# A delta-rule attention block on one core: the rounds of a head laid out by hand, with the build-time scheduler switched off

## The chip, the cores and the metric

The kernel runs on one core of a Trainium2 chip, in 32-bit floating point throughout. The metric is the time of one execution in microseconds, as the device reports it; the median of several runs is given. The profiled execution is one further run, taken by the hardware profiler. Engines are called PE (matrix multiplication, TensorE), DVE (VectorE), ACT (ScalarE), POOL (GpSimd) and SP (SyncE, which here issues most of the DMAs).

## The reference

The input x has 8 batches of 256 tokens with 256 channels. A modulation of a small vector c gives six rows per batch. Cut to what matters:

```
mod = silu(c) @ wmod                    # sa, ca, ga, sb, cb, gb per batch
h = layernorm(x) * (1 + ca) + sa
x = x + ga * attention(h)
h = layernorm(x) * (1 + cb) + sb
x = x + gb * (sparsify_2to4(silu(h @ w_gate) * (h @ w_up)) @ w_down)

# attention: 16 key heads, two value heads for each, 128 wide
q, k, v = causal_conv_4_taps(h @ W_qkv);  q, k = l2norm(q), l2norm(k)
for t in range(256):                    # state S of each value head, 128 x 128
    dv = beta[t] * (v[t] - k[t] @ S)
    S = S * decay[t] + outer(k[t], dv)
    o[t] = q[t] @ S
y = (rms_norm(o) * norm_w * silu(h @ W_z)) @ W_out
```

`sparsify_2to4` keeps, of every four neighbouring hidden values, the two that are largest in magnitude.

## The kernel before

The recurrence is solved in chunks of 128 tokens, two per batch. Within a chunk the influence of a key on later ones is a triangular matrix of 128 x 128, which is inverted in blocks of 32; with the inverse, a chunk becomes a few 128-wide matmuls.

The 8 batches are taken in four pairs, and for each pair the 16 key heads in four groups of four (`GH = 4`). So the main loop (from L1058) runs over 16 groups and 64 heads; each head serves both batches of the pair, both chunks and both value heads.

The work is written as generators, each of which issues some instructions on several engines and then yields:

- `attend` (L753 to L880), one for each batch of the pair, six steps. Values are transposed (`ps_v` L767) and scaled on ACT (`vn` L772); keys are multiplied with keys and queries (`ps_kq` L779 to L783), scaled on ACT (`cross` L786) and DVE (`aq` L788); then `ps_u` L798 with its copy `u` L800; `ps_ks` L806 with `rr` L811 on DVE and `o` L820 on ACT, and `ps_o` L825 with its copy L826; `ps_u1` L831 with L833; last `ps_o1` L837, added to `o` by DVE (L838). After that comes the normalisation: squares on ACT (`junk`, `ss` L845), a scaling on DVE (`ss` L848), a power of -1/2 on POOL (`rs`, in the helper at L105), and four products on DVE (`og` L861). It leaves behind a generator `turned` (L870) that waits five rounds, transposes `og` (`ps_gt` L877) and scales it (`og_p` L878).
- `levels` (L658 to L750), the inverse of the head that comes next, four steps: loads of its blocks by SP (`x_even` L675, the diagonal of `t_inv` L676, `x_top` L681, `low_up` L685), `ps_w` L691 with the copies `w` L699, `ps_t` L705 with the transpose `low` L713 on DVE and copies on ACT, `ps_w2` L731/L734 with `w2` L738, `ps_t2` L742/L745 with the copies into `t_inv`.
- `prepare` (L606 to L655), the query, the two values and two gates of the head that comes next: `ps_qv` L432 with a convolution of one ACT instruction (L418) and three of DVE (L420), `ps_z` L634 with a SiLU (L641), and the norm of the query (`ps_n2q` L447, with squares `junk` L451 on ACT ahead of it).
- `shares` (L891, `ps_y`, added up on DVE in L902), the output projection of two heads, once in two heads.
- `ahead`, called the background: keys, decays and triangular matrices of the next group (`ps_k` L432, `ps_n2k` L447, `diag` L516 on POOL, a scan L551, `ps_kk` L532, `a_t` L563), then the 30 solving steps `tmp` L592 and `xb` L598 on DVE.
- the feed: either `other_filled`, which makes the modulated tokens of a later pair (`ps_h` L147 and others), or `feed_forward` (L160 to L256) of one unit of 128 tokens of the pair before: `ps_ff` L190, SiLU L197, product `hid` L198, magnitudes L205, comparisons L211 to L224, mask `hid` L229, `ps_out` L244, result L252 and L253. The last four units come after the main loop and run one step each in turn.

The program has eight PSUM banks in three pools: three for projections and `ps_y` (`ps_in`), two for the inverse and the feed-forward (`ps_inv`), three for `attend` and the rest (`ps_mix`). A pool's next user waits until the bank's reader is done.

What sets the order of the work: in each head a list of generators is stepped round and round (L1105 to L1127), in the order `turned` of the head before, the older `shares`, `attend` of batch 0, `attend` of batch 1, `levels`, `prepare`. After each round `along` (L1073) steps the background as far as a planned share of its work, and then the feed. A head has 7 or 9 rounds, a group 32. This written order is not yet the program: the context that builds it is called with `schedule_with_timeline_sim=True` (L1201), with which instructions are reordered at build time by a simulated timeline, dependencies kept.

## Time and profile before

| | |
|---|---|
| median of 3 runs | 2168.65 us (2167.95, 2168.65, 2175.1) |
| profiled execution | 2163.81 us |
| its span in the profile | 2162.0 us |
| granted PE clock, mean | 0.987 of full speed |
| instructions in the profile | 46431 |
| moved by DMA | 226.85 MB, 105 GB/s in the mean |
| POOL, largest groups | `rs` L105 135.2 us in 128 instructions, `diag` L516 122.8 us in 64 |

The profile calls an engine busy from the start of an instruction to its end. Matmuls are pipelined on PE, so that one begins before the last has ended, and their ends are modelled; weight loads are counted apart, as PEld. A wait is put down to the instruction that released it last ("releaser"). An entry such as `L105` is a line of the kernel, and `out<-in` gives the names of the tiles that an instruction writes and reads.

### The profile page before, as it was taken

Reading aid. Unit: us, or ns where it says so; the run is one execution under the profiler, and the core shown is the slowest. Engines: PE = TensorE matmul, PEld = TensorE weight load, DVE = VectorE, ACT = ScalarE, POOL = GpSimd, SP = SyncE. Lnnn points to the kernel's source line nnn. Section 1 sums busy time; section 2 is a strip of 40 time slices with the busy share of each in tenths; the row PEclk is TensorE's granted clock in tenths of the full one; section 3 lists DMA queues with packets and bytes.
Section 4 is the critical chain, followed back from the end, with each engine's and each line's share of the span. In section 5 each row is a group of like instructions: output and inputs, shape, how many; then the busy total and the mean of one; then the engine's idle time right before and its main releaser. Section 6 shows DMA issues by size and latency. Waiting matters only on the chain.

```text
span 2162.0 us, 46431 instructions
## 1 busy us (share of the span) xinstructions
PE 2061.9 (95%) x16684; PEld 1634.1 (76%) x16684; DVE 1663.1 (77%) x4039; ACT 1373.6 (64%) x4552; POOL 370.7 (17%) x375
## 2 busy tenths in 40 slices
PE   8889999999999999999999999999999989999998
PEld 5567777777777777778777787787878777787887
DVE  6688686877869578797878868788797868879457
ACT  3577676866656566666566656666676666666652
POOL 3120212112120111212121121211202012121010
PEclk9999999999999999999999999999999999999999
DMA  4242423333342443434434343443434344343336
GB/s 137 85 117 65 105 68 101 91 83 91 101 117 67 124 115 95 132 90 109 119 90 118 104 109 94 122 117 87 132 92 108 92 115 120 108 113 90 75 91 212
DMA packets 324517, 226.85 MB, mean 105 GB/s; under 512 B 254520, under 2 KB 266168, under 8 KB 324288
## 3 DMA queue, kind: packets, MB, share of 16 engines
q1 hardware_dynamic: 304416, 163.34, 28.2%
q10 hardware_dynamic: 19872, 60.54, 8.8%
q8 instruction: 133, 2.18, 0.4%
q14 instruction: 96, 0.79, 0.1%
HBM read 186.28 MB, written 29.12 MB: 100 GB/s over the span
## 4 chain that ended last, share of the span: by engine, by line
PE 64%; ACT 12%; DVE 11%; DMA 7%; issue 4%; SPq 1%; POOL 1%; ACTq 0%; DVEq 0%; POOLq 0%
PE ps_y L891 9%; PE ps_qv L432 8%; PE ps_z L634 8%; PE ps_ks L806 5%; PE ps_ff L190 3%; PE ps_k L432 3%; PE ps_o L825 2%; PE ps_u L831 2%; DVE cv L420 2%; PE ps_out L244 2%; DMA blk<-scr 2%; PE ps_kk L532 2%; DMA scr<-a_t 2%; PE ps_u L798 2%; DVE a_t L563 2%
## 5 line engine op out<-in xcount | busy, mean ns | idle before, releaser
L420 DVE SCALAR_TENSOR_TENSOR cv<-ps_qv,conv_sb,cv 128x510 f32<-128x510 f32 (+1 forms) x564 | 410.2, 737 | 43.5 <-ACT cv L418 39.4
L432 PE MATMUL ps_qv<-h_bp,wh 128*128 128x512 f32 x768 | 365.1, 601 | 12.0 <-ACT junk L451 8.4
L105 POOL TENSOR_TENSOR rs<-ss,minus_halves 128x4 f32<-128x4 f32 x128 | 135.2, 1058 | 1019.6 <-DVE ss L848 1018.6
L634 PE MATMUL ps_z<-wh,h_bp 128*128 128x256 f32 x1024 | 250.4, 390 | 9.5 <-ACT junk L451 6.6
L891 PE MATMUL ps_y<-wo,og_p 128*128 128x256 f32 x1024 | 236.8, 380 | 0.8 <-ACT og_p L878 0.8
L432 PEld LDWEIGHTS ps_qv<-h_bp,wh 128*128 128x128 f32 x768 | 133.3, 191 | 118.9 <-issue 99.3
L634 PEld LDWEIGHTS ps_z<-wh,h_bp 128*128 128x128 f32 x1024 | 189.1, 193 | 38.5 <-ACT junk L451 9.9
L891 PEld LDWEIGHTS ps_y<-wo,og_p 128*128 128x128 f32 x1024 | 187.4, 190 | 22.8 <-ACT og_p L878 1.1
L418 ACT ACTIVATE cv<-ps_qv,conv_sb 128x512 f32<-128x512 f32 x188 | 129.6, 690 | 117.6 <-PE ps_qv L432 117.0
L592 DVE TENSOR_TENSOR tmp<-blk,xb 128x30 f32<-128x30 f32 (+14 forms) x480 | 156.8, 327 | 57.8 <-ACT xb L586 48.7
L516 POOL TENSOR_TENSOR diag<-consts,bk 128x1032 f32<-128x1032 f32 x64 | 122.8, 1919 | 384.5 <-DVE bk L507 352.6
L845 ACT ACTIVATE junk<-o 128x128 f32<-128x128 f32 x512 | 153.3, 303 | 41.4 <-DVE o L838 35.0
L551 DVE TENSOR_TENSOR_SCAN e<-dbc,diag 128x1032 f32<-128x1032 f32 x60 | 137.9, 2298 | 39.3 <-POOL diag L516 36.3
L598 DVE TENSOR_TENSOR xb<-xb,tmp 128x30 f32<-128x30 f32 (+14 forms) x480 | 157.0, 327 | 9.5
L420 DVE SCALAR_TENSOR_TENSOR k_t<-ps_k,conv_sb,k_t 128x510 f32<-128x510 f32 (+1 forms) x189 | 139.7, 740 | 24.8 <-ACT k_t L418 22.9
L861 DVE SCALAR_TENSOR_TENSOR og<-o,rs,gz 128x128 f32<-128x128 f32 x512 | 145.9, 344 | 10.3 <-POOL rs L105 8.1
L772 ACT ACTIVATE vn<-ps_v,nk 128x256 f32<-128x256 f32 x256 | 106.2, 483 | 61.4 <-PE ps_v L767 61.2
L806 PE MATMUL ps_ks<-u,cross 128*128 128x128 f32 x1024 | 141.0, 280 | 0.9 <-ACT u L800 0.9
L806 PEld LDWEIGHTS ps_ks<-u,cross 128*128 128x128 f32 x1024 | 130.8, 194 | 9.5 <-issue 3.3
L190 PE MATMUL ps_ff<-h,w_ff 128*128 128x128 f32 x1024 | 130.0, 277 | 3.2 <-ACT h L149 2.2
L190 PEld LDWEIGHTS ps_ff<-h,w_ff 128*128 128x128 f32 x1024 | 122.5, 192 | 7.8 <-ACT h L149 3.2
L432 PE MATMUL ps_k<-h_bp,wk 128*128 128x512 f32 x256 | 124.9, 613 | 1.6 <-ACT junk L451 1.2
(177 smaller groups left out, 4274.8 us busy)
## 6 DMA issues: line engine op xcount, KB each, us to landing
wh<-in_w_heads ACTq DMA_DIRECT2D x64, 640.0 KB, 4.0
w_ff<-in_w_ff SPq DMA_DIRECT2D x128, 256.0 KB, 2.9
dbc<-d_dram SPq DMA_DIRECT2D x60, 516.0 KB, 4.3
wo<-in_w_heads ACTq DMA_DIRECT2D x32, 512.0 KB, 3.7
w_dn<-in_w_down SPq DMA_DIRECT2D x64, 256.0 KB, 3.8
wk<-in_w_keys SPq DMA_DIRECT2D x16, 512.0 KB, 4.5
scr<-a_t SPq DMA_DIRECT2D x256, 32.0 KB, 2.6
blk<-scr SPq DMA_DIRECT2D x16, 512.0 KB, 3.6
```

The lines of the kernel that those rows point to most:

```text
L105: nc.gpsimd.tensor_tensor(out=out, in0=in_, in1=minus_halves[:, :n], op=ALU.pow)
L190: nc.tensor.matmul(ps[:, a, l, :], lhsT=w[:, k, l, :], rhs=h2[:, k, :], start=(k == 0), stop=(k == CC - 1),)
L420: nc.vector.scalar_tensor_tensor(out=dst[:, :, d:], in0=ps[:, :, : T - d], scalar=taps[:, KC - 1 - d : KC - d], in1=dst[:, :, d:], op0=ALU ...
L432: nc.tensor.matmul(ps.rearrange("p b t -> p (b t)"), lhsT=w[k], rhs=h_bp[:, k, :], start=(k == 0), stop=(k == CC - 1),)
L551: nc.vector.tensor_tensor_scan(e.rearrange("p i s t -> p (i s t)"), dbc.rearrange("p i f -> p (i f)"), diag.rearrange("p s t -> p (s t)"), ...
L592: nc.vector.tensor_tensor(out=tmp, in0=blk[:, j, j + 1 :, None].to_broadcast([P, m, j]), in1=xb[:, j, None, 0:j].to_broadcast([P, m, j]), ...
L598: solved = nc.vector.tensor_tensor(out=xb[:, j + 1 :, 0:j], in0=xb[:, j + 1 :, 0:j], in1=tmp, op=ALU.subtract)
L634: nc.tensor.matmul(ps[:, n, :], lhsT=h_bp[:, k, i * T + n * P : i * T + (n + 1) * P], rhs=wh[:, k * 640 + 384 : (k + 1) * 640], start=(k = ...
L806: nc.tensor.matmul(ps_ks[:, ct, h, :], lhsT=cross[:, h, ct, :], rhs=u0[:, h, :], start=True, stop=True)
L845: nc.scalar.activation(junk, o[:, n, h, :], AF.Square, accum_out=ss[:, n, h : h + 1])
L861: nc.vector.scalar_tensor_tensor(out=og[:, n, h, :], in0=o[:, n, h, :], scalar=rs[:, 2 * n + h : 2 * n + h + 1], in1=gz[:, i, n, h, :], op ...
L891: nc.tensor.matmul(ps_y[:, n, :], lhsT=og_p[:, j // 2, i, n, j % 2, :], rhs=wo[:, j // 2, j % 2, :], start=(j == 0), stop=(j == 3),)
```

## The change

Two things are changed. The build-time scheduler's flag is set to False, and the order of a round is written anew. The generators of a head are now stepped in this order: `attend` of batch 0, `levels` (called `inverse`), `prepare` (called `queries`), `attend` of batch 1, the background, the feed, and last `turned` of the head before with the older `shares`. To allow that, `along` is divided into `next_group` and `feeding`, which `shares_of` turns into endless generators; the loop ends when all the others are used up.

```
-            def along():
-
-                nonlocal done, rounds, fed
+            def next_group():
+
+                nonlocal done, rounds
                 rounds += 1
                 while done < work * rounds / (total * 3 / 4):
...
+            def feeding():
+
+                nonlocal fed
                 while fed < (FEED_STEPS + LATER) * rounds / total:
...
-                turns, ends[:] = ends[:], []
+                turned, ends[:] = ends[:], []
                 if hp % 2 == 0:
-                    turns.append(waiting)
+                    turned.append(waiting)
...
-                turns += [attend(rec, i, *shared, t_inv[head % 2], og_p[:, hp % 2, i]) for i in range(2)]
+                atts = [attend(rec, i, *shared, t_inv[head % 2], og_p[:, hp % 2, i]) for i in range(2)]
...
-                    turns.append(levels(coming[0], *coming[1], t_inv[(head + 1) % 2]))
+                    inverse = levels(coming[0], *coming[1], t_inv[(head + 1) % 2])
...
-                        gen, shared = begin(to_come["kh"], to_come["bp"], to_come["h"])
-                        turns.append(gen)
-                while turns:
-                    with tc.issue_after(first_solved) if head == 0 else ExitStack():
-                        turns = [t for t in turns if next(t, turns) is not turns]
-                    along()
+                        queries, shared = begin(to_come["kh"], to_come["bp"], to_come["h"])
+                turns = [atts[0], inverse, queries, atts[1], shares_of(next_group), shares_of(feeding), *turned]
+                left = {id(t) for t in (*turned, *atts, inverse, queries)}
+                while left:
+                    for t in turns:
+                        with tc.issue_after(first_solved) if head == 0 else ExitStack():
+                            if next(t, turns) is turns:
+                                left.discard(id(t))
...
-    with tile.TileContext(nc, schedule_with_timeline_sim=True) as tc:
+    with tile.TileContext(nc, schedule_with_timeline_sim=False) as tc:
```

The number of instructions of each engine is the same in both programs, and so is the number of rounds of each head. In the built programs the order differs on every engine; counted as runs of equal neighbours, PE has 3246 rows before and 3355 after, DVE 3410 and 3618, ACT 2365 and 2394, POOL 323 and 365, SP 748 and 823. With the flag at False the built order is still not letter for letter the written one. An example from PE of the changed program, where four matmuls of one norm, 32-wide blocks of an inverse and a projection, each written in one piece, stand mixed:

```
L447 n2k x1
L691 ps_w x1
L447 n2k x3
L432 ps_k x1
L691 ps_w x15
```

More of the change, by code (lines that the diff above doesn't have):

```diff
@@ L1055, in later, with shares_of @@
             yield from gen
+        def shares_of(work):
+            while True:
+                yield work()
         og_p = wo = shared = None
@@ L1094, in adaln_block @@
                     for _ in levels(rec, *scratch, t_inv[head % 2]):
-                        along()
-                turns, ends[:] = ends[:], []
+                        next_group()
+                        feeding()
+                turned, ends[:] = ends[:], []
                 if hp % 2 == 0:
-                    turns.append(waiting)
+                    turned.append(waiting)
                     og_p = two.tile([P, 2, 2, NCH, 2, P], F32, tag="og_p", name="og_p", bufs=1)
@@ L1108, in adaln_block @@
                     waiting = shares(ya, k0 + hp == 0, og_p, wo, 6)
-                turns += [attend(rec, i, *shared, t_inv[head % 2], og_p[:, hp % 2, i]) for i in range(2)]
+                atts = [attend(rec, i, *shared, t_inv[head % 2], og_p[:, hp % 2, i]) for i in range(2)]
                 solved, coming = False, None
+                inverse = queries = iter(())
                 if hp + 1 < GH:
@@ L1118, in adaln_block @@
                     solved = True
-                    turns.append(levels(coming[0], *coming[1], t_inv[(head + 1) % 2]))
+                    inverse = levels(coming[0], *coming[1], t_inv[(head + 1) % 2])
                     if head > 0:
                         to_come = coming[0]
-                        gen, shared = begin(to_come["kh"], to_come["bp"], to_come["h"])
-                        turns.append(gen)
-                while turns:
-                    with tc.issue_after(first_solved) if head == 0 else ExitStack():
-                        turns = [t for t in turns if next(t, turns) is not turns]
-                    along()
+                        queries, shared = begin(to_come["kh"], to_come["bp"], to_come["h"])
[6 more added lines that the diff above has]
+                                left.discard(id(t))
                 head += 1
```

## The prediction

> **What bounds the kernel now.** I read the busy row first, then the shares of the chain that ended last, then PE's timeline inside one head, then PE's and DVE's waits, last the tail.

> ```profile
> PE 2061.9 (95%) x16684; PEld 1634.1 (76%) x16684; DVE 1663.1 (77%) x4039; ACT 1373.6 (64%) x4552; POOL 370.7 (17%) x375
> PE 64%; ACT 12%; DVE 11%; DMA 7%; issue 4%; SPq 1%; POOL 1%; ACTq 0%; DVEq 0%; POOLq 0%
> ```

> TensorE (PE) looks full, yet only 64% of the chain lies on it; ACT and DVE carry 23% and DMA 7%. The timeline of PE settles which of the two to believe:

> ```profile
> 1001.36 3.62 PE L891 MATMUL ps_y<-wo,og_p 128*128 128x256 f32 x16
> 1004.81 1.88 PE L432 MATMUL ps_k<-h_bp,wk 128*128 128x512 f32 x4
> 1006.53 0.60 PE L767 MATMUL ps_v<-consts,cv 128*128 128x128 f32 x4
> 1007.06 0.69 PE L691 MATMUL ps_w<-x_even,a_t 32*32 32x32 f32 x32
> ```

> A row's first column is its start, the second its length. Each row ends after the next has begun: 16 matmuls of 256 columns take 3.45 us from start to start, 216 ns each, where the page gives 380 as the mean of one. By starts I find 430 ns for 512 columns, 216 for 256, 111 for 128, 109 for transposes and norms, 20 and 29 for the 32- and 64-wide blocks. With the counts of the groups: 1024 x 430 + 2560 x 216 + 5120 x 111 + 1600 x 109 + 4096 x 20 + 2048 x 29 ns = 440 + 553 + 568 + 174 + 82 + 59 = 1,876 us; with some 30 us at the start for the first loads, about 1,910. So PE loses some 250 us of the 2,162, where its busy row leaves 100. [...] It matters for this sum: by the busy row a better order could win 100 us at the very most, by the starts up to 250, so a large gain can't be ruled out from "95%". About half of the lost time I find in named waits, about half in pieces of 0.1 us at changes of operand without a releaser. The named ones:

> ```profile
> PE ps_kq L779 <- ACT vn L772: 16.0, 11, 3.0
> PE ps_qv L432 <- ACT junk L451: 8.4, 10, 1.2
> PE ps_z L634 <- ACT junk L451: 6.6, 10, 0.9
> PE ps_w L731 <- ACT x_top L720: 4.2, 5, 1.3
> PE ps_t L705 <- ACT w L699: 2.3, 5, 0.6
> PE ps_t L705 <- DMA t_inv<-scr_y: 2.2, 2, 1.3
> PE ps_out L244 <- DVE hid L229: 0.2, 1, 0.2
> ```

> (us in all, times, longest.) They are few and short; the last rows are links that today hardly wait at all.

> **The change part by part.** No instruction is added or taken out: every engine has the same count of each kind, so PE's 1,910 us stand. What moves is order, and the built order of the changed program can be read. It is not the order written: neighbours still come mixed (four columns of one norm between pieces of an inverse), so I cost the built order. Method: for each link from a producer to a PE instruction I add up PE's work (durations above) that stands between them before and after, and compare it with the link's measured need. Sums are made against the profiled execution, 2163.81 us (span 2162.0 and 1.8 around it); the median shown, 2168.65, lies 4.8 above it.

> *What goes.* The norms of query and key no longer hold the three projection banks just ahead of L432 and L634: 8.4 + 6.6 + 1.2 = 16 us of waits on L451, between 0 and -20; I take -16. The second batch's ps_kq stands a whole turn of inverse and queries after its values: of the 16.0 us of L779, 0 to -16; the first batch's place is as tight as before, so -6.

> *The gap at POOL.* The normalisation goes DVE L848, POOL L105 (1,058 ns, 128 times), DVE L861. Today DVE works meanwhile:

> ```profile
> 1044.86 0.15 DVE L848 SCALAR_TENSOR_TENSOR ss<-ss,eps_q 128x4 f32<-128x4 f32 x1
> 1044.98 0.22 DVE L592 TENSOR_TENSOR tmp<-blk,xb 128x58 f32<-128x58 f32 x1
> 1045.23 0.22 DVE L598 TENSOR_TENSOR xb<-xb,tmp 128x58 f32<-128x58 f32 x1
> 1045.49 0.24 DVE L592 TENSOR_TENSOR tmp<-blk,xb 128x84 f32<-128x84 f32 x1
> 1045.77 0.25 DVE L598 TENSOR_TENSOR xb<-xb,tmp 128x84 f32<-128x84 f32 x1
> 1046.14 1.14 DVE L861 SCALAR_TENSOR_TENSOR og<-o,rs,gz 128x128 f32<-128x128 f32 x4
> ```

> Four solve steps fill the 1.13 us, so the wait of L861 on POOL sums to 8.1 us only. In the built order 115 of the 128 places have under 1 us of DVE work between L848 and L861 (half of them none): DVE idles some 85 us more. Queued behind each waiting L861 are the conv (L420) and the additions L838, for whose banks PE waits. DVE is only 77% busy, so most costs nothing; it tells where DVE's work per head exceeds PE's. After the change that is the fourth head of each group (DVE 21 us, PE 19). There 16 heads x 2 gaps x 0.9 = 28 us; half of it reaches PE: +14, between 0 and +60.

> *The feed-forward's output.* L244 needs the masked hidden L229. Before, 0.2 us. In the built order 8 of the 12 units inside the loop have 13.3 us of DVE work queued from the last transpose L713 to L229, and PE 11.4 us until L244: 8 x 1.9 = +15; overlapping with the gap above I take +10 for this and +12 for POOL's, bounds 0 and +25.

> *The tail.* The last four units run alone, with two banks:

> ```profile
> 2132.32 10.98 PE L190 MATMUL ps_ff<-h,w_ff 128*128 128x128 f32 x96 [0.92 <-DVE hid L198]
> 2143.74 5.45 PE L244 MATMUL ps_out<-w_dn,hid 128*128 128x256 f32 x24 [0.44 <-DVE hid L198]
> 2149.38 8.90 PE L244 MATMUL ps_out<-w_dn,hid 128*128 128x256 f32 x40 [0.19 <-DVE hid L229]
> ```

> PE waits 1.5 us here. In the built order eight of the masks L229 stand in one block ahead of five of the products L198 that free the banks: 4.9 us of DVE work against banks already used up. And from the last L198 to the first unit's own last L229 lie 6.5 us of DVE work against 1.7 us of PE work (eight matmuls of L244): another 4.8. Some of it stands before too, so +8, between +3 and +12. Such a gap has a second price. [...] In this trace PE is idle 5.12 us before L470 at 62.30, and the granted clock reads 0.76 in 60:64, 0.81 in 64:68 and 1.00 after: 0.24 x 4 + 0.19 x 4 = 1.7 us lost. By the row 1.7 for a gap of 5 us, [...] I add 2 for the tail, which makes it +10. [...]

> *The inverse.* PE work between the copy w (L699) and L705 is under 1.2 us in 19 of 64 heads (11 before), between w2 (L738) and its products (L742) in 20 (5 before). 23 more tight places at about 0.25 us, the mean of the rows above being 0.5: +6 (0 to +12). The inverse's loads: L676 lands 1.9 us after issue in the median, queued on SP behind others; the cover of L705 falls below 4 us in 24 heads, none before. At 0.2 each +5 (0 to +15).

> *Banks of the attention.* From the last addition L838 to the bank's next user PE now has under 1 us of work in 43 heads (never under 2 before), and DVE needs 0.5 to 1.45: 43 x 0.12 = +5 (0 to +25). In exchange the conv's banks get longer cover (5.6 us at the fifth percentile, 3.7 before), which is in the -16 already.

> *More changes.* PE's rows of equal neighbours grow from 3,246 to 3,355. At 0.05 us, the loss without a releaser over the rows: +5 (0 to +14).

> *The start.* The modulation copy L406, which must wait for PE's L399 (10.25 us), comes ahead of some of the statistics, so xs L137 and the first transposes L147 slip: +2 (0 to +4).

> Sum: -16 - 6 + 12 + 10 + 10 + 6 + 5 + 5 + 5 + 2 = +33. 2163.8 + 33 = 2196.8; the median of such runs lies up to 4.8 higher. I say 2199.

> **The rivals.** *DVE becomes the bound.* The 85 us of gaps and the fourth heads' 21 against 19 us add up instead of hiding: every group hands a lag on. With the upper ends for POOL's gap (+60), the output (+25), the banks (+15) and the rest as above the sum is +90: about 2250. For it: 77% busy over the span, and DVE's queue runs in the order built. Against: in the other three heads of a group PE has 5 to 12 us more work than DVE, and the lag is caught up.

> *Faster.* Spreading the two batches' steps round the inverse and the queries lets each eviction hide, and of the 125 us of unnamed small losses and the 50 us named a part vanishes: -22 for what I name, and a fifth of the rest, -25, with the costs above at their lower ends (about +10): 2163.8 - 37, about 2130. It decides if DVE never lags more than the 2 to 3 us cover it has; the longer cover of u0 (2.2 to 2.6 us at the lower quartile) and of the gates (2.6 to 4.1) speak for it, the thinner covers above against.

> *It does not do what it says.* Part of the order is still the builder's, the counts and rounds are the same, and gains and losses cancel: 2168, plus or minus 6.

> **How the numbers follow.** About 0.3% is what a measurement can tell from no change: 2162.1 to 2175.2. The sum of the terms 0.50, DVE as the bound 0.22, no change 0.11, faster 0.17. The likeliest case alone spans 2178 to 2225 (the terms' bounds, not all at one end). The range reaches from 2150, inside the faster case, to 2255, the DVE case's middle and a little: some 2 in 10 stay outside. Faster 0.17, same 0.11, slower 0.72.

> **What would show it.** PE's waits on junk L451 all but gone; og L861 on POOL's rs up from 8.1 to some 90 us; new PE rows ps_out on hid L229 (about 15 us), ps_ff on hid L198 in the tail, ps_v on o L838, ps_t on w L699 and on t_inv; a clock slice under 1.00 in the tail; ps_h starting near 13 us, not 11.40. Wrong if L861's row stays near 10, or if PE's idle without a releaser shrinks while the named rows stay as short as before.

## The result and the profile after

The changed kernel takes 2249.41 us in the median of four runs (2239.8 to 2255.21), beside 2169.48 for the kernel before on the same chips (2167.95 to 2175.1): 1.0359 times as long, with an interval of 1.0318 to 1.0400. It is 80 us slower; the sum of the forecast was 33. Its profiled execution took 2255.21 us, with a span of 2253.1, so 91 us of span are to be explained, beside the 2162.0 of before.

The busy row of the page for the changed kernel:

```profile
PE 2112.9 (94%) x16684; PEld 1650.6 (73%) x16684; DVE 1639.7 (73%) x4039; ACT 1357.6 (60%) x4552; POOL 368.6 (16%) x375
```

The counts of PE, DVE, ACT and POOL are those of before. PE's busy time has grown by 51 us without one more matmul, which already says that "busy" is not work: the same matmuls took longer, or their ends were held back. The chain of this trace could be followed over 13% of the span only, so I don't use it.

PE's waits in the changed kernel (us in all, times, longest):

```profile
PE ps_n2k L447 <- DVE k_t L420: 22.1, 15, 2.0
PE ps_out L244 <- DMA w_dn<-in_w_down: 16.1, 8, 4.0
PE ps_u L831 <- ACT o L820: 13.9, 11, 2.2
PE ps_u L798 <- ACT vn L772: 8.8, 7, 2.2
PE ps_t L705 <- ACT w L699: 7.2, 3, 4.2
...
PE ps_qv L432 <- ACT junk L451: 1.7, 4, 0.4
PE ps_k L432 <- ACT junk L451: 1.2, 1, 1.2
```

The first three of them in the kernel before:

```profile
PE ps_u L831 <- ACT o L820: 0.6, 1, 0.6
...
PE ps_out L244 <- DMA w_dn<-in_w_down: 0.5, 2, 0.3
PE ps_n2k L447 <- DVE k_t L420: 0.5, 1, 0.5
```

The waits of before are gone: L779 on vn (16.0 us) is not in the list at all, the three on junk L451 (16 us) are down to 2.9. In their place stand others that come back at one place of nearly every group: the norm of the fourth key (15 waits in 15 of the 16 groups), the feed-forward's weights (8 in 12 units). The bank that ps_u1 takes from ps_ks adds 11 waits.

DVE's timeline round one normalisation (L848 and L861 are the scaled sum and the products; the bracket is the idle time ahead, and its releaser):

```profile
1070.78 0.16 DVE L848 SCALAR_TENSOR_TENSOR ss<-ss,eps_q 128x4 f32<-128x4 f32 x1
1072.06 1.14 DVE L861 SCALAR_TENSOR_TENSOR og<-o,rs,gz 128x128 f32<-128x128 f32 x4 [1.12 <-POOL rs L105]
```

Where four solve steps filled the 1.13 us before, DVE now stands idle, and a second time right behind (1.15 us ahead of 1074.42). The list of DVE's waits sums it, first in the changed kernel, then in the kernel before:

```profile
DVE o L838 <- PE ps_o L837: 118.0, 56, 6.8
DVE og L861 <- POOL rs L105: 105.6, 104, 1.2
```

```profile
DVE o L838 <- PE ps_o L837: 42.6, 24, 4.0
...
DVE og L861 <- POOL rs L105: 8.1, 12, 1.1
```

The tail of PE in the changed kernel:

```profile
2196.11 13.61 PE L190 MATMUL ps_ff<-h,w_ff 128*128 128x128 f32 x116
2216.17 13.00 PE L190 MATMUL ps_ff<-h,w_ff 128*128 128x128 f32 x96 [6.45 <-DVE hid L198]
2229.00 3.62 PE L244 MATMUL ps_out<-w_dn,hid 128*128 128x256 f32 x16
2236.64 12.31 PE L244 MATMUL ps_out<-w_dn,hid 128*128 128x256 f32 x48 [4.03 <-DVE hid L229]
```

The two waits forecast at 4.9 and 4.8 are 6.45 and 4.03 us. And the same 96 matmuls that took 10.98 us take 13.00, right behind the wait. Why they do is told by the windows of the profile: length, busy time of PE with its number of instructions, and PE's granted clock (the last two columns are of the DMAs).

```profile
1052.00:1056.00 4.00, 2.34 (x27) 1.00 0.56 153
1056.00:1060.00 4.00, 3.90 (x16) 0.57 0.19 33
1060.00:1064.00 4.00, 4.00 (x35) 1.00 0.13 21
...
2212.00:2216.00 4.00, 0.00 (x0) 0.70 0.07 27
2216.00:2220.00 4.00, 3.83 (x18) 0.50 0.14 44
```

The first three rows lie round one wait of 1.76 us on the fourth key (PE goes on at 1056.10): in the next four microseconds PE is busy for 3.90 and gets through 16 instructions, at a clock of 0.57. A clock of 0.50 stands in the records in stretches of 3.41 us or a multiple, called half-clock windows below: 57 us in all before, 103 after.

With the trace's start times all 91 us can be sorted. From each PE instruction to the next I take off the time that its shape needs at full speed (the durations of the forecast) and put what is left into one of four classes: over 150 ns with a releaser that the trace names; a change of tile size on PE (128 to 32 or 64 wide or back); within a stretch at half clock; the rest. In us, with the number of size changes and of half-clock windows of 3.41 us:

| kernel (its profiled span) | named waits | half clock | size changes | rest |
|---|---|---|---|---|
| before (2162) | 114 | 22 (17) | 58 (550) | 36 |
| changed (2253) | 158 | 43 (30) | 67 (624) | 54 |
| difference | +44 | +20 | +9 | +18 |

PE's work is 1,921 us in both, close to the 1,910 of the forecast. Half of the loss is waits with a name. Nearly a quarter is a slower clock behind such waits, for which the forecast had 2 us.

### The profile page after: what moved, and what is told of

Read it like the earlier page. It is cut to its first block, busy times and chain, and to the rows that moved or that the text cites. A ratio compares the mean times of both kernels' runs of the same rounds, so it can differ in the third digit from the quotient of the medians.

```text
span 2253.1 us, 46385 instructions
## 1 busy us (share of the span) xinstructions
PE 2112.9 (94%) x16684; PEld 1650.6 (73%) x16684; DVE 1639.7 (73%) x4039; ACT 1357.6 (60%) x4552; POOL 368.6 (16%) x375
## 5 line engine op out<-in xcount | busy, mean ns | idle before, releaser
L420 DVE SCALAR_TENSOR_TENSOR cv<-ps_qv,conv_sb,cv 128x510 f32<-128x510 f32 x564 | 416.4, 739 | 55.8 <-ACT cv L418 53.5
L432 PE MATMUL ps_qv<-h_bp,wh 128*128 128x512 f32 x768 | 386.1, 615 | 3.9 <-DVE y L902 2.2
L105 POOL TENSOR_TENSOR rs<-ss,minus_halves 128x4 f32<-128x4 f32 x128 | 133.6, 1044 | 1020.7 <-DVE ss L848 1020.7
L634 PE MATMUL ps_z<-wh,h_bp 128*128 128x256 f32 x1024 | 257.9, 394 | 0.0
L861 DVE SCALAR_TENSOR_TENSOR og<-o,rs,gz 128x128 f32<-128x128 f32 x512 | 153.8, 347 | 117.3 <-POOL rs L105 105.6
L891 PE MATMUL ps_y<-wo,og_p 128*128 128x256 f32 x1024 | 234.2, 384 | 0.0
L891 PEld LDWEIGHTS ps_y<-wo,og_p 128*128 128x128 f32 x1024 | 193.2, 193 | 33.0 <-ACT og_p L878 5.9
L516 POOL TENSOR_TENSOR diag<-consts,bk 128x1032 f32<-128x1032 f32 x64 | 122.8, 1918 | 554.3 <-DVE bk L507 546.8
L634 PEld LDWEIGHTS ps_z<-wh,h_bp 128*128 128x128 f32 x1024 | 188.9, 196 | 24.8 <-issue 0.9
L772 ACT ACTIVATE vn<-ps_v,nk 128x256 f32<-128x256 f32 x256 | 107.2, 476 | 148.5 <-PE ps_v L767 148.3
L432 PEld LDWEIGHTS ps_qv<-h_bp,wh 128*128 128x128 f32 x768 | 127.6, 192 | 82.0 <-issue 67.3
L592 DVE TENSOR_TENSOR tmp<-blk,xb 128x30 f32<-128x30 f32 (+14 forms) x480 | 156.3, 326 | 15.1 <-ACT xb L586 12.0
L598 DVE TENSOR_TENSOR xb<-xb,tmp 128x30 f32<-128x30 f32 (+14 forms) x480 | 156.7, 327 | 3.5
L420 DVE SCALAR_TENSOR_TENSOR k_t<-ps_k,conv_sb,k_t 128x510 f32<-128x510 f32 (+2 forms) x189 | 135.7, 734 | 31.0 <-ACT k_t L418 30.1
L838 DVE TENSOR_TENSOR o<-o,ps_o 128x256 f32<-128x256 f32 x128 | 53.1, 419 | 122.8 <-PE ps_o L837 118.0
L190 PE MATMUL ps_ff<-h,w_ff 128*128 128x128 f32 x1024 | 129.7, 280 | 10.3 <-DVE hid L198 6.5
L190 PEld LDWEIGHTS ps_ff<-h,w_ff 128*128 128x128 f32 x1024 | 123.1, 195 | 18.9 <-DVE hid L198 7.3
L432 PE MATMUL ps_k<-h_bp,wk 128*128 128x512 f32 x256 | 132.5, 619 | 4.2 <-ACT gz L641 3.0
```

The lines of the kernel that those rows point to most:

```text
L105: nc.gpsimd.tensor_tensor(out=out, in0=in_, in1=minus_halves[:, :n], op=ALU.pow)
L190: nc.tensor.matmul(ps[:, a, l, :], lhsT=w[:, k, l, :], rhs=h2[:, k, :], start=(k == 0), stop=(k == CC - 1),)
L420: nc.vector.scalar_tensor_tensor(out=dst[:, :, d:], in0=ps[:, :, : T - d], scalar=taps[:, KC - 1 - d : KC - d], in1=dst[:, :, d:], op0=ALU ...
L432: nc.tensor.matmul(ps.rearrange("p b t -> p (b t)"), lhsT=w[k], rhs=h_bp[:, k, :], start=(k == 0), stop=(k == CC - 1),)
L592: nc.vector.tensor_tensor(out=tmp, in0=blk[:, j, j + 1 :, None].to_broadcast([P, m, j]), in1=xb[:, j, None, 0:j].to_broadcast([P, m, j]), ...
L598: solved = nc.vector.tensor_tensor(out=xb[:, j + 1 :, 0:j], in0=xb[:, j + 1 :, 0:j], in1=tmp, op=ALU.subtract)
```

## The experiments

Theory A: the flag is the cause. Without the simulated timeline each engine's order has fixed places in every group where too little lies between producer and consumer, and the half clock follows the waits. Theory B: one of these, DVE idle on POOL ahead of L861, makes DVE the bound. Theory C: the new layout of the round is the cause. Ratios are to the kernel before, run on the same chip, with their intervals.

**Flag and layout apart.** One kernel has the round as before and the flag at False:

```
-    with tile.TileContext(nc, schedule_with_timeline_sim=True) as tc:
+    with tile.TileContext(nc, schedule_with_timeline_sim=False) as tc:
```

> The round written as before, only the scheduler's flag set to False. Theory A (the loss is the flag's: without the simulated timeline DVE's L861 stands right behind L848, loads and evictions stand at fixed, too short distances in every group): as slow as the changed kernel or slower, 2240 to 2300 us, with L861's wait on POOL at some 105 us again (the built order has under 1 us of DVE work in 124 of the 128 gaps). Theory C (the loss is the new layout's: both batches apart, the background in the middle): close to before, 2165 to 2190. If the layout makes good a part of what the flag costs, this is slower than 2249.

The other has the new layout and the flag left at True.

> The new layout of a round with the scheduler's flag left at True. Theory A: within 1% of before, 2155 to 2190 us, L861's wait on POOL well under 105 us (the built order fills 55 of the 128 gaps with over 1 us, against 80 before), and few gaps of PE over 1.2 us. Theory C: near the changed kernel, 2225 to 2255.

The flag alone: 2239.41 us, 1.0337 (1.0295 to 1.0379), as slow as the changed kernel within the intervals. The layout alone: 2149.99, 0.9919 (0.9886 to 0.9951), faster than before. C is out: the layout wins 0.8% with the scheduler, and without it the two layouts can't be told apart. The flag is what costs: 3.4% on the old layout, 4.4% on the new one (1.0359 by 0.9919). By the classes of the table the flag alone has 151, 39 (29 windows), 68 and 60, the layout alone 108, 20 (15), 57 and 37. The waits of DVE in the kernel with the flag alone, then in that with the layout alone:

```profile
DVE og L861 <- POOL rs L105: 119.8, 124, 1.2
```

```profile
DVE og L861 <- POOL rs L105: 36.0, 36, 1.2
```

So POOL's place ahead of L861 is a mark of the flag too. In the kernel with the flag alone the chain that ended last can be followed over the whole span:

```profile
PE 51%; DVE 24%; ACT 9%; DMA 7%; POOL 4%; issue 4%; SPq 1%; ACTq 0%; POOLq 0%; DVEq 0%
```

Before it was PE 64%, DVE 11% and POOL 1%. So with the flag off DVE stands on the chain for a quarter of the time, though it is busy for only 73% of the span; POOL itself takes a small part. Whether POOL's place is what costs, the next runs ask.

**DVE and POOL.** First attempt, one yield ahead of the products:

```
+            yield
             og = mixp.tile([P, NCH, 2, P], F32, tag="og", name="og", bufs=2)
```

> The changed kernel with one yield ahead of the four products L861, so that they are written a turn later than POOL's power and DVE has other work between. Theory B (DVE is the bound, fed by its idle time on POOL): L861's wait falls from 105.6 us to under 40, and the time by 30 to 60 us, to about 2200. Theory A (DVE's idle time on POOL is mostly slack; PE loses at other places, a few us each, and by the lower clock after each): the wait falls as much, the time by less than 15 us, 2235 to 2250.

2243.78 us, 1.0358 (1.0324 to 1.0393). It says nothing for or against: the wait was still 102.6 us in 108 places (104 in the changed kernel), so in these places of the built order, which with the flag off is not the written one either, too little work stood between the power and the products. Second attempt, the power left out:

```
-            rs = small.tile([P, NS], F32, tag="rs", name="rs")
-            rsqrt(rs, ss.rearrange("p n h -> p (n h)"))
+            rs = ss.rearrange("p n h -> p (n h)")
```

> The changed kernel without POOL's power of -1/2 on the sums of squares (L861 multiplies by the scaled sum itself; the power is left out of the computation), so that DVE's L861 has nothing to wait for behind L848. The yield of the run before did not do that: L861's wait stayed at 102.6 us. Theory B (DVE's idle time on POOL, 105.6 us, is what makes PE late): 30 to 60 us less, about 2200. Theory A (it is slack, PE loses at fixed places of the order and by the half clock behind them): less than 15 us, 2235 to 2250.

2209.45 us, 1.0211 (1.0187 to 1.0234): some 32 us less than the changed kernel by the ratios. B holds for about that much, so far as this edit can tell. In the profile the named waits fall from 158 to 130 and the half clock from 43 to 21 (30 windows to 15). The wait that shrank most, from 13.9 us:

```profile
PE ps_u L831 <- ACT o L820: 3.4, 6, 0.7
```

DVE still has 26% of the chain here: the power is one cause of DVE's lateness, not the whole of it.

Third, the power kept and the products held back in DVE's order:

```
+            yield
...
+            latest = next(
+                i for i in reversed(nc.cur_bb.bb.instructions) if i.engine == nc.vector.engine
+            )
...
+                    with tc.issue_after(latest):
```

> The changed kernel with POOL's power kept, and the products L861 written a turn later and queued on DVE behind the last instruction written there before them, which the first such run lacked. Nothing is left out. Theory B (DVE's idle time on POOL): L861's wait falls from 105.6 us to under 45 and the time as it did without the power, ratio 1.018 to 1.025, about 2210. If leaving out the power helped for another reason (128 fewer instructions on POOL, diag L516 sooner): the wait falls, the time does not, ratio over 1.030. If the products come so late that ps_gt waits for them: slower than the changed kernel.

2228.76 us, 1.0278 (1.0262 to 1.0293): 17 us less, half of what leaving the power out gives, and between the two expectations. DVE's waits in this kernel (the products are now L866):

```profile
DVE o L838 <- PE ps_o L837: 58.7, 27, 5.6
DVE o L838 <- ACT u L833: 52.8, 13, 4.7
...
DVE og L866 <- POOL rs L105: 4.0, 11, 0.9
```

The wait on POOL is gone, and L838 now waits 52.8 us for ACT, which it hardly did in the changed kernel (1.9): part of the idle time has only moved. Other things moved as well: the waits of L244 on w_dn, which stay at 15.8 us without the power, are down to 1.2 here. So the 17 us are not POOL's alone, and what POOL's latency costs PE is known roughly: about 32 us by the one edit, 17 with others mixed in by the other. A fourth kernel is the same edit with the new layout and the flag on.

> The new layout with the scheduler's flag on, and the products L861 a turn later as above. The layout alone gave 0.992 with L861 waiting 36 us for POOL. If that wait still costs: 0.985 to 0.991, the best so far. If the scheduler has already hidden it: 0.990 to 0.998.

2214.77 us, 1.0209 (1.0193 to 1.0225), outside both expectations and 2.9% slower than the layout alone, although the wait on POOL fell from 36.0 to 2.7 us. A wait that the layout alone does not have now heads PE's list, and the half-clock windows go from 15 to 29:

```profile
PE ps_o L825 <- ACT o L820: 17.7, 8, 3.3
```

So a shorter wait on POOL is no gain if the new order makes others late. Whether the 36 us cost anything with the scheduler on, this run cannot tell. The control, the power left out of the kernel before:

> The kernel before, with POOL's power left out as above. There DVE waited only 8.1 us for POOL in all, so both theories expect little: 0 to -8 us. The difference to the -32 us of the same edit in the changed kernel is then what the order makes of the same instruction. If this falls by 15 us or more, POOL's latency costs in either order (its share of the chain was 1%), and the -32 does not tell what the change did.

2179.00 us, 1.0053 (1.0034 to 1.0072), slower, which neither theory expected. The named waits are the same (114), PE's work too, size changes +4; the half clock is 35 us in 24 windows instead of 22 in 17. I read two things from it. The gain of 32 us belongs to the changed order, not to POOL as such. And an edit lets the whole order be built anew, which alone can move the time by half a per cent (11 us), here by the clock; the 17 and 32 us above carry an uncertainty of that size.

**Weights and tail.** Four buffers for the feed-forward's weights in the loop (`w_bufs=4`):

> The changed kernel with four buffers for the feed-forward's weights instead of three inside the loop, so that the fourth load of w_down needs not wait for the first two matmuls L244. Theory A: the waits of L244 on w_dn (16.1 us in 8 units) go, and the low clock behind some of them (about 1 us each): -16 to -25 us, about 2230. Theory B: PE only waits elsewhere for DVE, so -0 to -8 us.

2243.81 us, 1.0347 (1.0319 to 1.0375), not to be told from the changed kernel. The waits of L244 on w_dn are gone; those of L691 on x_even grew from 2.9 to 9.5 us and of L831 from 13.9 to 17.4. With the last four units started two turns apart as well:

```
+    units = [behind(u, 2 * j) for j, u in enumerate(units)]
     while units:
         units = [u for u in units if next(u, units) is not units]
```

> The changed kernel with the last four feed-forward units started two turns behind one another instead of in step, and four weight buffers inside the loop. Theory A: the two waits of the tail (6.45 us on hid L198, 4.03 on hid L229) and the half clock behind them go, about -12, and the waits on w_dn as in the run with four buffers, -5: 2230 to 2237. If the tail is bound by DVE's total work, the waits only change place: 2240 to 2247.

2223.73 us, 1.0284 (1.0261 to 1.0307), 16 us less. From the first transposes of the tail to the end it is 50.8 us, beside 65.9 in the changed kernel (from 2187.19) and 54.0 before (from 2107.98). The tail of PE in this kernel:

```profile
2183.22 14.86 PE L190 MATMUL ps_ff<-h,w_ff 128*128 128x128 f32 x128
2197.92 3.71 PE L244 MATMUL ps_out<-w_dn,hid 128*128 128x256 f32 x16
2201.47 3.73 PE L190 MATMUL ps_ff<-h,w_ff 128*128 128x128 f32 x32
2205.04 10.53 PE L244 MATMUL ps_out<-w_dn,hid 128*128 128x256 f32 x48
```

No bracket is left, and 48 matmuls of L244 take 10.53 us, not 12.31: DVE's work is the same, so it was the order, not DVE's speed, that the tail waited for.

**The fourth key and the clock.** Idle matmuls ahead of the norm were to keep PE busy through its wait, so that the clock's price shows by itself:

```
+            for n in range(warm):
+                nc.tensor.matmul(ps[:, n % 2, 0, :], lhsT=ident, rhs=ident, start=True, stop=True)
```

> The changed kernel with 14 idle matmuls of 128 columns (1.55 us) ahead of the norm of each group's fourth key (ps_n2k), where PE waits 1.4 to 2 us for DVE in nearly every group; they are overwritten. 15 x 1.55 = 23 us of work are added in place of 22 us of waits. If the half clock behind such waits costs what the records say (6 of the 21 stretches at half speed follow this wait, each 3.41 us, up to 1.7 us lost): 2249 + 1 - 10 = about 2240, with 14 to 16 stretches left. If the clock does not matter, or the waits only move: 2249 to 2260.

2311.65 us, 1.0691 (1.0664 to 1.0717). The half-clock windows fell from 30 to 19 and their loss from 43 to 25 us, but PE had 47 us more of work and the named waits rose to 182. The count was wrong by a factor of two: each of the 14 calls is two instructions. With fewer:

> As the run with idle matmuls, with 6 calls in place of 14. A call of 128 columns turned out to be two instructions of 111 ns, so that the 14 were 3.1 us, longer than the wait they stand in, and 46.6 us of work in all. Now 1.33 us in 15 places, 20 us of work, less than the wait of 22. If the half clock behind this wait costs time: 2249 + 20 - 20 - 6 to 10, about 2241, with 22 to 25 windows of half clock (30 in the changed kernel's profile). If a shift of PE's order by a microsecond costs more than that, as the +60 of the run with 14 may say: 2255 to 2285.

2273.32 us, 1.0500 (1.0467 to 1.0532), with 27 windows. The profile says why this could not work:

```profile
PE ps_n2k L446 <- DVE cv L420: 23.5, 15, 2.1
```

L446 is the idle matmul itself. It reads only a constant, so it can wait for nothing but its bank, whose last reader is another convolution on DVE; and it waits as long as the norm did. Behind the wait on k_t that the list of the changed kernel shows there stood a second one, nearly as long, which the list could not show. So these two runs did not fill the wait, and do not tell the clock's price. Next, the norm of that key a turn later:

```
+                if hp == GH:
+                    yield 3.0
```

> The changed kernel with one empty step of the background ahead of the last three steps of each group's fourth key, so that its norm (ps_n2k) is written a turn after DVE's convolution of that key. If that wait is a loss of its own (22.1 us of waits in 15 groups, and 6 of the stretches at half speed): the row goes under 8 us and the time falls by 15 to 30 us, to some 2225. If it only shows that DVE is late at that place of a group: the wait comes back at the next instruction that needs DVE, and the time stays within 8 us of 2249.

2264.19 us, 1.0451 (1.0428 to 1.0474), slower by 0.9%. The row of ps_n2k fell from 22.1 to 0.9 us, others rose (L731 on x_top from 3.0 to 16.9, L634 on DVE's cv from nothing to 11.1): the waits came back elsewhere, some of them on DVE.

**Edits together.** Power out, tail and buffers, key later:

> The changed kernel with three of the edits together: POOL's power left out (as in the run without it), the staggered tail with four weight buffers, and the fourth key's norm a turn later. If the losses are separate and add up: the ratios to before go 1.036 - 0.015 - 0.0075 - (0 to 0.012), about 1.005 to 1.013, or 2173 to 2192 us beside 2163. If they have one cause (DVE late), they overlap, and the time stays over 2200.

2180.08 us, 1.0053 (1.0033 to 1.0074). Without the key:

> The changed kernel with POOL's power left out, the staggered tail and four weight buffers, but the fourth key's norm where it was. Alone the ratios to before were 1.021 and 1.028 beside 1.036, and 1.045 for the norm a turn later; all three together gave 1.005. If the losses add up: 1.036 - 0.015 - 0.0075 = 1.0135, about 2196 us beside 2167. If they share a cause (one late place takes the cover of the next, and the half clock multiplies it), the two together win more than their sum: 1.005 to 1.010, and the norm's place matters little.

2187.59 us, 1.0087 (1.0073 to 1.0101). And without leaving out the power:

> The changed kernel with the staggered tail, four weight buffers and the fourth key's norm a turn later, POOL's power kept. If the losses add up: 1.028 + 0.009 = 1.037. If the norm's later place only hurts where DVE idles on POOL, as three together say: still 1.030 to 1.040. If it helps once the weights are not late: under 1.025.

2223.82 us, 1.0251 (1.0232 to 1.0269). Power with tail and buffers takes 2.7% off, where the sum of the two alone is 2.2. The later key costs 0.9% alone; beside each of the others it seems to win 0.3%, but there the intervals touch. Three edits bring back 0.031 of the 0.036, one of them by leaving out a step of the computation. Their classes are 115, 14 (9 windows), 64 and 51 us: the named waits are those of before, and the clock is better.

**The best of the parts.** New layout, flag on, staggered tail, four buffers:

> The new layout with the scheduler's flag on, the staggered tail and four weight buffers: the best of the parts so far. Theory A: 2140 to 2150 us, 1% under before, since with the simulated timeline there are few waits left for the buffers to take away. If the hand order only gets in the scheduler's way in the tail: 2150 to 2160.

2148.97 us, 0.9936 (0.9915 to 0.9957), no better than the layout alone. With the scheduler on there was little left for these buffers. The fastest version is the new layout with the flag left on, at 0.992.

## Why the prediction was right and wrong

The direction, the range and about half of the mechanisms were right; the size was wrong, 33 us in place of 80 by the medians and 91 by the profiles. In the classes of the table the sum reads:

| | forecast | measured |
|---|---|---|
| named waits (all other terms) | +26 | +44 |
| half clock | +2 | +20 |
| small losses ("more changes") | +5 | +27, 9 of them at size changes |

So three steps failed: DVE's idle time was taken to cost nothing outside the fourth heads, the half clock was priced only for a long gap, and the small losses were sized at 5 us instead of 27. Term by term:

- *What goes*: -16 on junk L451 became -13, and -6 on L779 became -16. Right, a little too small.
- *The gap at POOL*: DVE's idle time came as forecast (some 90 us; 105.6). The step that failed is the next: "DVE is only 77% busy, so most costs nothing", and "half of it reaches PE" in the fourth heads, taken as +12. Without the power it was 32 us less, half clock included. I asked where DVE's work per head exceeds PE's. But DVE need not have more work than PE: with the flag off it stands on the chain for 24% of the time at 73% busy. It is enough that something PE needs next stands behind the idle microsecond. DVE took nothing ahead of a waiting L861: in ten places of the changed kernel a solve step L598 stands behind it whose operand is written when the wait begins, and it begins only after the products (at 1110.15 us, behind a wait from 1108.96 to 1109.88). Without the power L831's wait for its bank fell from 13.9 to 3.4 us and that of the fourth key's norm from 22.1 to 18.3. By which instructions of DVE and ACT the delay went on, no run shows.
- *The half clock*: "I add 2 for the tail". The records show +20, ten times the term. I priced the clock only for gaps of about 5 us, like the one of 5.12 us before L470, and so found one. The trace of before held the answer: 57 us at half clock, with only one PE gap over 3.1 us after the first load. In the changed kernel the half clock followed 9 of the 29 windows of 3.41 us in which PE was idle for 1.2 to 2.0 us, and all ten with more (the last section has the count). So a wait that I counted at its length alone was on average too cheap.
- *The feed-forward's output*: +10 for L229 inside the loop. It did not come; L244 waited 16.1 us there for its weights, which I had not costed at all: a load of w_dn takes 3.6 us in the median from issue to landing, and w_dn shares three buffers with w_ff. With four buffers the wait was gone, which won little by itself.
- *The tail*: +10 forecast; from the first transposes of the tail to the end 11.9 us more. Right, and shown by the staggered tail.
- *The inverse*: +6 for w and w2, and +5 for the loads. w to L705 grew by 5.8 us. The loads did not cost: L705's wait on t_inv, 2.2 us before, is gone.
- *Banks of the attention*: +5, by L838. A bank wait came, by another reader: L831 on o L820 from 0.6 to 13.9.
- *More changes*: +5. Size changes went from 550 to 624 and cost 9 more; a change of line alone has a median cost of 0. Another +18 us of small losses at full clock stand in no term of the forecast, and their cause stays open.
- *The start*: ps_h at 13.75 us, forecast near 13. Right.
- Not foreseen: the fourth key's norm, 22.1 us. It is DVE late at one place of each group.

The rival that DVE becomes the bound gave 2250, and the time was 2249, but that is luck: with the upper ends it names its sum comes to +106, about 2270, not to +90; its +60 for POOL's gap is twice what any run shows, and no edit on DVE alone brings back more than 32 of the 80. That the change does not do what it says was half true: the order is still the builder's, which is why the single yield did nothing. The hand layout's gain, which the faster rival spoke of, exists, 0.8% with the flag on; switching the flag off took 4.4% from that layout.

What stays open: the +18 us of small losses at full clock, and how the losses share among causes, since they overlap (the edits' gains don't add up, and each edit has the order built anew, which moved the time by 0.5 to 0.9% in the control and in the run with the later key). The half clock's share rests on the clock's records and on the control, not on a run that changes the clock alone.

## What to carry to other kernels

When an order changes, price a new wait on an engine by who stands behind it in that queue, not by whether the engine has time to spare on average; and look for waits that come back at one place of every round. Before counting a PE wait at its length, look in the trace of before what idle time the half clock already follows: there, 9 of the 18 windows of 3.41 us in which PE was idle for 1.2 to 2.0 us, and all three with more. And test a layout and the switch that reorders it apart: here one gains and the other loses, and the sum hides both.

## What the runs showed of the hardware

| PE idle in the window | windows | half clock next |
|---|---|---|
| under 0.8 us | 10,297 | 1 |
| 0.8 to 1.2 us | 382 | 14 |
| 1.2 to 2.0 us | 385 | 123 |
| 2.0 us and more | 134 | 134 |

- In the third row it followed 84 of the 128 windows in which eight or more matmuls of 32 or 64 wide started, and 39 of the other 257; why, no run shows. So idle time of the same length had no half clock behind it in 262 of the 385 windows, and one in 123. A window at half clock cost 1.3 to 1.6 us by the sorting above (22 us in 17 before, 43 in 30 in the changed kernel, 14 in 9 with three edits together).
- A change between 128-wide and 32- or 64-wide matmuls took extra time on PE: 91 to 95 ns on the way to the small ones, 100 to 102 back from 32-wide and 118 to 120 back from 64-wide (medians by pair of lines). Between 128-wide matmuls of different lines the median is 0 (1,568 steps at full clock in the trace of before, those over 150 ns with a releaser left out).
- An idle matmul call of 128 columns in 32-bit stands as two PE instructions: the run with 14 of them has 210 calls more, 420 instructions more in its page (17104 beside 16684), and 47 us more work. A transpose stands as one: the 512 calls of L767 are 512 instructions.
